# Longer attention rings, earlier batch norm rows and earlier routing breaks in a four-layer graph network

## The chip, the cores and the metric

The kernel runs on one core of one Trainium2 chip. A core has five engines that run side by side, each through its own list of instructions in order: TensorE (PE, with its weight loads as PEld), VectorE (DVE), ScalarE (ACT), GpSimd (POOL) and SyncE (SP). SP issues the plain transfers, GpSimd the gathers and scatters by index. The metric is the device time of one launch in microseconds (us), the median of the runs.

## The reference

Four layers work on x, 3125 tokens by 256 columns (f32, 25 tiles of 128 rows). Each layer does

    xn = layernorm(x)
    x  = x + gnn(xn, edges) + mix(xn)
    x  = x + ffn(...)

with a different gnn, mix and ffn each time. Two pieces matter here. Layer 1's gnn is graph attention with 4 heads of 64 columns over 50000 edges: per edge a score, a softmax over the edges of a destination, and a weighted sum of the source rows. Layer 3's ffn has 4 experts of hidden width 512; which two experts a token uses, and with what weight, comes out of another graph attention, with 4 heads of 4 columns over 32768 edges of its own:

    h     = (x @ W_gat) as (tokens, 4 heads, 4 experts)
    e     = leaky_relu(a_src[src] + a_dst[dst]); alpha = softmax of e over the edges of a dst
    agg   = segment_sum(h[src] * alpha, dst) + b_gat
    score = layernorm(agg).mean over heads; w = softmax of the best 2
    x     = x + sum over experts of w * (gelu(xn @ W1 + b1) @ W2 + b2)

Layers 2 and 3 have a batch norm over all tokens at the end of their gnn, before relu and the addition to x.

## The kernel before, in words

**Edges come in chunks of 128**, sorted by destination: 391 chunks for the graph, 256 for the routing list. For each chunk GpSimd gathers the 128 source rows from DRAM into SBUF by one indirect transfer, VectorE makes a one-hot matrix of destinations (E, L455), and TensorE adds one-hot times rows into a PSUM bank (L459, to_windows). When the last chunk that touches a tile of 128 tokens is in, the tile is closed.

**Attention with a ring (gat_near, from L832).** Gathered rows live in a ring of RING = 35 chunk slots. Iteration i of the generator asks for chunk i (L892), and works chunk i - late, late = 30: it multiplies the rows by their softmax weight (L904) and sums them. Between the two, scores are worked in batches of 16 chunks (CB): batch b starts at iteration 16b + 24, 8 after its last row is asked for, and takes six steps, one per iteration: scores plus leaky relu (L856, L858, DVE), a transpose (L862, PE), two running maxima along the sorted edges (L868, L870, DVE), a transpose back (L879, PE), exp (L884, ACT). A gather may overwrite a slot only when the sum of the chunk that was there, 35 earlier, is done. The running maxima need "breaks": penalties of -2^100 wherever the destination changes (breaks, L787), computed from a list of destinations in DRAM (dlin) with 4 SP loads per 5 batches (L803) and two VectorE instructions (L805, L806).

**Order of work.** A generator yields pieces, and drive() takes turns between generators: (gat_near, 4), (experts, 3) means four iterations of the ring, then three steps of the experts. GpSimd's instructions keep the order of the program. The other engines' instructions are ordered when the kernel is built, by readiness and by place in the program, and what stands inside an If cannot move out of it.

**The last stage (tail_regular, L2299)** runs inside such an If. It holds, in program order: small loads; bn_end (scale and shift of the batch norm from the sums); breaks for the routing list; l3_near_setup; bn_apply, which per group of up to four tiles loads the normalised-to-be rows of the batch norm from DRAM into xn (L1034), scales, shifts, adds them to x (L1036 to L1039), layer-norms and transposes the group, and through fill() makes its 24-column rows (L116 with wg), writes them to DRAM (l3rows, the table the ring gathers from) and scatters the destination scores (l3seed); 12 steps of the experts; the spread of destination scores along the edges (spread, L824, L827); 40 more steps; and then ring and experts in turn. The groups go in the order 16, 20, 24, 0, 4, 8, 12 (first tile); tiles 16 to 24 have no routing edges, so their gates are known at once.

**The experts (l3_near_ffn, L2240)** go through the token groups in that order. For each expert there are 4 steps of hidden layer (product, Gelu on ACT, L2264) and one output step per tile (product, then x += gate * product on DVE, L2275), then the bias (L2289 to L2294). Before the output steps of a group the generator waits, in program order, until the group's gates are there (ready). The last group (12) keeps its products and adds them when its gates come.

**Layer 3's gnn stage** drives seg_near (gather and sum of 391 chunks, 2 per round), l3_mix (1 per round) and route_check (1 per round), which after 12 rounds loads the sorted routing list, writes its destinations to dlin2 and tests that the list has the regular form; the test decides the If.

Of the kernel before, what the change touches and what calls it, by code (L numbers as in the profile page):

```python
# [38 lines left out]
RING = 35  # L39
# [61 lines left out]
class Net:  # L101
# [685 lines left out]
    def breaks(self, pool, dlin, n):  # L787
# [10 lines left out]
        with self.tc.tile_pool(name="br", bufs=1) as tmp:  # L798
            for b0 in range(0, nb, 5):
                k = min(5, nb - b0)  # L800
                dh = tmp.tile([4 * CB, 5, w], F32, name="dh", bufs=2)[:, :k]
                for h in range(4):
                    nc.sync.dma_start(dh[h::4],  # L803
                                      self.lin(dlin, b0 * CB * P, [[P, CB], [CB * P, k], [1, w]]))
                nc.vector.tensor_tensor(pen[:, b0:b0 + k, 1:w], dh[:, :, 1:], dh[:, :, :w - 1], op=OP.not_equal)  # L805
                nc.vector.tensor_scalar(pen[:, b0:b0 + k, 1:w], pen[:, b0:b0 + k, 1:w], -BIG, None, op0=OP.mult)  # L806
            w = P + HALO
            dh = tmp.tile([per, 4, w], F32, name="dhc")
            nc.sync.dma_start(dh, self.lin(dlin, 0, [[P, per], [per * P, 4], [1, w]]))
            nc.vector.tensor_tensor(penc[:, :, 1:], dh[:, :, 1:], dh[:, :, :w - 1], op=OP.not_equal)  # L810
            nc.vector.tensor_scalar(penc[:, :, 1:], penc[:, :, 1:], -BIG, None, op0=OP.mult)
# [20 lines left out]
    def gat_near(self, pool, g, table, pre, pen, d, close):  # L832
# [5 lines left out]
        n, late = g["n"], CB + 14  # L838
        f = d + 2
        nb = -(-n // CB)  # L840
        ring = pool.tile([P, RING, 4, f], F32, name="ring")
        att = pool.tile([P, nb * CB + 2, 4], F32, name="att")
        ex = pool.tile([P, nb * CB, 4], F32, name="ex")
        nc.vector.memset(att, 0.0)

        def spans(c0, c1):
            while c0 < c1:
                e = min(c1, c0 - c0 % RING + RING)
                yield c0, e, ring[:, c0 % RING:c0 % RING + e - c0]
                c0 = e  # L850

        def batch(b):
# [31 lines left out]
            nc.scalar.activation(ex[:, c0:c0 + CB, :], dif, AF.Exp)  # L884
# [5 lines left out]
        for i in range(n + late):  # L890
            if i < n:
                nc.gpsimd.indirect_dma_start(out=ring[:, i % RING].rearrange("p h f -> p (h f)"), out_offset=None,  # L892
                                             in_=table,
                                             in_offset=bass.IndirectOffsetOnAxis(ap=g["src"][:, i:i + 1], axis=0))
            for b in range(nb):
                if i == min(b * CB + CB, n - 1) + 8:
                    live.append(batch(b))
# [4 lines left out]
            if c >= 0:  # L902
                r = ring[:, c % RING]
                nc.vector.tensor_mul(r[:, :, :d + 1], r[:, :, :d + 1],  # L904
                                     ex[:, c, :, None].to_broadcast([P, 4, d + 1]))
# [122 lines left out]

    def bn_apply(self, b, sc, sh, then=None, order=GROUPS):

        nc = self.nc
        for t0, n in order:
            h = self.xn[:, t0:t0 + n, :]
            nc.sync.dma_start(h, b["h"][t0 * P:(t0 + n) * P, :].rearrange("(t p) f -> p t f", p=P))  # L1034
# [1077 lines left out]
    def route_check(self, pool, table, ok):  # L2112

        nc = self.nc
        for _ in range(12):
            yield
# [10 lines left out]
        self.none_bad(pool, bad, ok)  # L2127

# [170 lines left out]
    def tail_regular(self, sorted_r, bn, gb):  # L2299
# [4 lines left out]
        with tp("g3") as gp, tp("ffn3") as fp, Banks(self, mm=4, ga=2, seg=2):  # L2304
            r = gp.tile([P, T, 4], F32, name="r")
            nodeg = gp.tile([P, T], F32, name="nodeg")
            par = {n: self.rowb(gp, "L3_ffn_" + n) for n in ("b_gat", "ln_gamma", "ln_beta")}
# [3 lines left out]
            sc, sh = self.bn_end(bn, fp, *gb)  # L2311
            pen, penc = self.breaks(gp, self.dlin2, C2)
            with tp("set4") as p:
                g, rows_d, aself, gin, pre, fill, end = self.l3_near_setup(gp, p, sorted_r)
                nc.vector.tensor_scalar(nodeg, self.deg2, 0.5, -BIG, op0=OP.is_lt, op1=OP.mult)

                def gate(t0, n):
                    self.l3_gates(gp, gin, par, r, t0, n)
                    ready.add(t0)

                def then(t0, n):
                    fill(t0, n)
                    if t0 >= T2:
                        gate(t0, n)
                self.bn_apply(bn, sc, sh, then, GROUPS[4:] + GROUPS[:4])
                for _ in range(12):
                    next(experts)
            with tp("spread4") as p:
                end(p, penc)
            for _ in range(40):  # L2330
# [7 lines left out]
            drive((self.gat_near(gp, g, rows_d, pre, pen, 4, close), 4), (experts, 3))  # L2338
# [146 lines left out]
    def fast(self):  # L2485
# [3 lines left out]
        with tc.tile_pool(name="keepf", bufs=1) as keep, tc.tile_pool(name="dramf", bufs=1, space=DRAM) as dram:  # L2489
# [41 lines left out]
            with tp("att1") as gp:  # L2531
# [13 lines left out]
                with Banks(self, mm=2, acc=2, ga=2, seg=2), tp("mix1") as mp:  # L2545
                    close = self.gat_close(gp, table, 64, aself, nodeg, 1e-12, add_x)
                    drive((self.gat_near(gp, g, table, pre, pen, 64, close), 4), (self.l1_mix_lean(mp), 1),
# [27 lines left out]
            with Banks(self, **norms), tp("bn2") as bp:  # L2575
                with tp("gl2") as gp:
# [10 lines left out]
                    sc, sh = self.bn_end(bn, bp, self.rowb(gp, "L2_gnn_gamma"), self.rowb(gp, "L2_gnn_beta"))  # L2587
                self.bn_apply(bn, sc, sh)
# [20 lines left out]
            with tp("bn3") as bp:  # L2609
                gb = [self.rowb(bp, "L3_gnn_" + k) for k in ("gamma", "beta")]  # L2610
                bn = self.bn_start(bp)
                with Banks(self, **norms):
                    with tp("gl3") as gp, tp("mix3") as mp, tp("chk4") as cp:
                        drive((self.seg_near(gp, g, tab, g["src"], self.l3_close(gp, own, bn)), 2),
                              (self.l3_mix(mp, self.xnT), 1), (self.route_check(cp, by_dst, ok4), 1))
# [5 lines left out]
                with branch.Else():  # L2621
                    with Banks(self, **plain), tp("end3") as p:
                        self.bn_apply(bn, *self.bn_end(bn, p, *gb))
# [262 lines left out]
```

## Time and profile before

| | |
|---|---|
| runs before | 5095.69, 5095.82, 5095.60 us; median 5095.69 |
| profiled execution | 5092.92 us, span 5091.2 us |
| granted TensorE clock, mean | 0.798 |
| busy: PE, DVE, ACT, POOL | 3585.0, 2165.8, 879.8, 2586.8 us |
| layer 1's ring: first and last gather | 1230.4, 1821.4 us |
| last stage: first expert loads to the end | 4318.8 to 5091.2 us |
| routing ring: first and last gather | 4415.8, 4997.3 us |

How to read it: an engine's busy time is a mean over stages that are limited by different things, so the stretches that the change touches are read one by one: what each engine did there, and what ended its idle time. A line such as "L892 POOL DMA_INDIRECT ring<-l3rows,e2src x256 | busy, mean ns | idle <- releaser" names the line of the code, engine, operation, what is written from what, how often, the busy time, and the idle time just before these instructions with what ended most of it. "remote" and "issue" are waits whose cause the trace does not show. One TensorE product in f32 appears as two instructions.

### The profile page before, as it was taken

Reading aid. Unit: us, or ns where it says so; the run is one execution under the profiler, and the core shown is the slowest. Engines: PE = TensorE matmul, PEld = TensorE weight load, DVE = VectorE, ACT = ScalarE, POOL = GpSimd, SP = SyncE. Lnnn points to the kernel's source line nnn. Section 1 sums busy time; section 2 is a strip of 40 time slices with the busy share of each in tenths; the row PEclk is TensorE's granted clock in tenths of the full one; section 3 lists DMA queues with packets and bytes.
Section 4 is the critical chain, followed back from the end, with each engine's and each line's share of the span. In section 5 each row is a group of like instructions: output and inputs, shape, how many; then the busy total and the mean of one; then the engine's idle time right before and its main releaser. Section 6 shows DMA issues by size and latency. Waiting matters only on the chain. (4 is left out here: it accounts for less than half of the span.)

```text
span 5091.2 us, 45299 instructions
## 1 busy us (share of the span) xinstructions
PE 3585.0 (70%) x12927; PEld 2341.1 (46%) x12927; DVE 2165.8 (43%) x7507; ACT 879.8 (17%) x1815; POOL 2586.8 (51%) x2609
## 2 busy tenths in 40 slices
PE   8657655864765666675766669998677885585779
PEld 3345433542433434343555434555455553354556
DVE  3565321125676774574434342113544223423333
ACT  2010001110210111112201021221112221211222
POOL 0565665664677735443666624660454445305540
PEclk9878767975877877777877779999788987586779
DMA  3422323313433320012333310001233223300000
GB/s 142 125 86 79 92 76 109 98 50 108 129 93 97 101 58 17 15 47 69 97 98 111 107 32 7 14 9 42 82 87 91 72 75 91 85 6 13 12 11 10
DMA packets 231338, 349.01 MB, mean 69 GB/s; under 512 B 74144, under 2 KB 168151, under 8 KB 231080
## 3 DMA queue, kind: packets, MB, share of 16 engines
q0 software_dynamic: 108384, 219.50, 15.7%
q1 hardware_dynamic: 118280, 122.48, 7.7%
q10 hardware_dynamic: 4416, 4.01, 0.2%
q8 instruction: 110, 1.80, 0.1%
q14 instruction: 148, 1.21, 0.1%
HBM read 295.13 MB, written 50.61 MB: 68 GB/s over the span
## 5 line engine op out<-in xcount | busy, mean ns | idle before, releaser
L494 POOL DMA_INDIRECT G<-tab,e1src x391 | 381.1, 975 | 489.9 <-PE seg L459 211.5
L459 PE MATMUL seg<-G,E 128*128 128x257 f32 (+1 forms) x1564 | 472.2, 441 | 213.5 <-DVE E L455 77.1
L116 PE MATMUL mm<-xnT,w 128*128 128x512 f32 (+1 forms) x1232 | 550.2, 595 | 10.9 <-DVE x L1937 4.5
L370 POOL DMA_INDIRECT by_src<-rec,place x391 | 399.1, 1021 | 310.9 <-PE mm L116 204.5
L494 POOL DMA_INDIRECT G<-h_tab,gi x391 | 379.5, 971 | 347.0 <-DMA selfw<-in_L_gnn_self_W 122.9
L455 DVE TENSOR_SCALAR E<-iota_row,e1dl 128x128 f32<-128x128 f32 x1173 | 327.7, 300 | 509.6 <-PE seg L459 252.6
L892 POOL DMA_INDIRECT ring<-l1rows,e1src x391 | 434.8, 1112 | 157.6 <-issue 81.6
L459 PE MATMUL seg<-ring,E 128*128 128x264 f32 (+1 forms) x1294 | 385.4, 427 | 181.9 <-DVE E L455 79.6
L459 PEld LDWEIGHTS seg<-G,E 128*128 128x128 f32 x1564 | 323.4, 219 | 344.5 <-issue 170.5
L494 POOL DMA_INDIRECT G<-tab,e3src x391 | 384.1, 982 | 190.3 <-issue 77.2
L116 PE MATMUL mm<-w,hT 128*128 128x256 f32 (+1 forms) x1712 | 439.0, 409 | 29.9 <-ACT hT L1602 21.2
L892 POOL DMA_INDIRECT ring<-l3rows,e2src x256 | 243.1, 950 | 339.7 <-PE seg L459 125.2
L459 PEld LDWEIGHTS seg<-ring,E 128*128 128x128 f32 x1294 | 245.4, 236 | 299.6 <-DVE E L455 119.3
L116 PEld LDWEIGHTS mm<-w,hT 128*128 128x128 f32 (+1 forms) x1712 | 333.4, 201 | 104.0 <-ACT hT L1602 30.0
L370 POOL DMA_INDIRECT by_dst<-rec,place x256 | 251.5, 983 | 243.1 <-PE mm L116 184.5
L116 PEld LDWEIGHTS mm<-xnT,w 128*128 128x128 f32 x1232 | 240.2, 209 | 242.0 <-issue 222.6
L443 PE MATMUL seg<-G,E 128*128 128x256 f32 x1070 | 295.0, 428 | 56.1 <-issue 23.4
L443 PEld LDWEIGHTS seg<-G,E 128*128 128x128 f32 x1070 | 228.9, 218 | 110.1 <-issue 32.3
L431 DVE TENSOR_SCALAR E<-iota_row,e3dl,rec 128x128 f32<-128x128 f32 (+1 forms) x391 | 140.4, 383 | 285.5 <-PE seg L443 142.0
L171 PE MATMUL mm<-ident,xn 128*128 128x128 f32 x400 | 95.0, 398 | 172.9 <-DVE xn L191 103.6
L1762 DVE SCALAR_TENSOR_TENSOR x<-mm,l2t_r,x 128x256 f32<-128x256 f32 x150 | 69.8, 481 | 320.5 <-PE mm L116 282.3
L904 DVE TENSOR_TENSOR ring<-ring,ex 128x260 f32<-128x260 f32 (+1 forms) x647 | 192.7, 318 | 2.7 <-ACT ex L884 2.6
(738 smaller groups left out, 5414.7 us busy)
## 6 DMA issues: line engine op xcount, KB each, us to landing
w<-in_L_ffn_w SPq DMA_DIRECT2D x16, 1024.0 KB
h_tab<-htab_s SPq DMA_DIRECT2D x25, 512.0 KB
r_b<-rowa SPq DMA_DIRECT2D x64, 128.0 KB
bn_h<-c_h SPq DMA_DIRECT2D x50, 128.0 KB
G<-h_tab,gi POOLq DMA_INDIRECT x391
by_src<-rec,place POOLq DMA_INDIRECT x391
ring<-l1rows,e1src POOLq DMA_INDIRECT x391
G<-tab,e3src POOLq DMA_INDIRECT x391
```

Of the source, the lines that this page charges most:

```text
L116: m = self.nc.tensor.matmul(out, l, r, start=(i == 0), stop=(i == last))
L171: self.nc.tensor.transpose(p[:, i * P:(i + 1) * P], src(t0 + i)[:, k * P:(k + 1) * P], self.ident)
L370: return self.nc.gpsimd.indirect_dma_start(out=table, out_offset=bass.IndirectOffsetOnAxis(ap=idx, axis=0), in_=src, in_offset=None, bound ...
L431: self.nc.vector.tensor_scalar(e[:, :w], self.iota2[:, :w], g["dl"][:, c:c + 1], weight[:, c:c + 1], op0=OP.is_equal, op1=OP.mult)
L443: self.nc.tensor.matmul(A[t], e, rows_c, start=first, stop=last)
L455: nc.vector.tensor_scalar(e, self.iota_row, g["dl"][:, c:c + 1], None, op0=OP.is_equal)
L459: nc.tensor.matmul(A["sum"], e, rows_c, start=(c == 0 or window(c - 1, nt) != k), stop=last)
L494: nc.gpsimd.indirect_dma_start(out=ring[i % len(ring)][:, :D], out_offset=None, in_=table, in_offset=bass.IndirectOffsetOnAxis(ap=gidx[:, ...
L892: nc.gpsimd.indirect_dma_start(out=ring[:, i % RING].rearrange("p h f -> p (h f)"), out_offset=None, in_=table, in_offset=bass.IndirectOff ...
L904: nc.vector.tensor_mul(r[:, :, :d + 1], r[:, :, :d + 1], ex[:, c, :, None].to_broadcast([P, 4, d + 1]))
L1762: nc.vector.scalar_tensor_tensor(self.x[:, t, :], p, r[:, t, e:e + 1], self.x[:, t, :], op0=OP.mult, op1=OP.add)
```

## The change

- gat_near takes the size of the ring and the wait from last gather to scores as arguments: 44 slots and 10 in layer 1, 136 slots and 20 in layer 3's routing. late becomes CB + wait + 6: 32 and 42. The softmax weights (ex) live in three rotating tiles of one batch each, no longer in one tile for all.
- The loads of the batch norm's rows become a function, bn_rows. In the last stage it is called first, before bn_end; in layer 2 between bn_end and bn_apply.
- route_check waits no rounds; a new generator tail_setup waits 3 rounds, runs it, and after one more round runs the breaks of the routing list into tiles that live until the last stage, with one dh buffer instead of two.
- In the last stage 4 expert steps are taken after each of the groups 0, 4, 8, 12 of bn_apply (instead of 12 after all), and 24 after the spread (instead of 40).

```diff
-RING = 35
+RING = 44
-    def breaks(self, pool, dlin, n):
+    def breaks(self, pool, dlin, n, bufs=2):
...
-                dh = tmp.tile([4 * CB, 5, w], F32, name="dh", bufs=2)[:, :k]
+                dh = tmp.tile([4 * CB, 5, w], F32, name="dh", bufs=bufs)[:, :k]
...
-    def gat_near(self, pool, g, table, pre, pen, d, close):
+    def gat_near(self, pool, g, table, pre, pen, d, close, size, wait):
-        n, late = g["n"], CB + 14
+        n, late = g["n"], CB + wait + 6
-        ring = pool.tile([P, RING, 4, f], F32, name="ring")
+        ring = pool.tile([P, size, 4, f], F32, name="ring")
-        ex = pool.tile([P, nb * CB, 4], F32, name="ex")
+        EX = {}
...
-            nc.scalar.activation(ex[:, c0:c0 + CB, :], dif, AF.Exp)
+            EX[b] = pool.tile([P, CB, 4], F32, name="ex", bufs=3)
+            nc.scalar.activation(EX[b], dif, AF.Exp)
...
-                if i == min(b * CB + CB, n - 1) + 8:
+                if i == min(b * CB + CB, n - 1) + wait:
...
+    def bn_rows(self, b, order=GROUPS):
+        for t0, n in order:
+            self.nc.sync.dma_start(self.xn[:, t0:t0 + n, :],
+                                   b["h"][t0 * P:(t0 + n) * P, :].rearrange("(t p) f -> p t f", p=P))
     def bn_apply(self, b, sc, sh, then=None, order=GROUPS):
             h = self.xn[:, t0:t0 + n, :]
-            nc.sync.dma_start(h, b["h"][t0 * P:(t0 + n) * P, :].rearrange("(t p) f -> p t f", p=P))
...
     def route_check(self, pool, table, ok):
-        for _ in range(12):
-            yield
...
+    def tail_setup(self, keep, table, ok):
+        for _ in range(3):
+            yield
+        with self.tc.tile_pool(name="chk4", bufs=1) as pool:
+            self.route_check(pool, table, ok)
+        yield
+        self.tail = self.breaks(keep, self.dlin2, C2, 1)
...
     def tail_regular(...):
-        with tp("g3") as gp, tp("ffn3") as fp, Banks(self, mm=4, ga=2, seg=2):
+        pen, penc = self.tail
+        with tp("ffn3") as fp, tp("g3") as gp, Banks(self, mm=4, ga=2, seg=2):
+            order = GROUPS[4:] + GROUPS[:4]
+            self.bn_rows(bn, order)
+            sc, sh = self.bn_end(bn, gp, *gb)
...
-            sc, sh = self.bn_end(bn, fp, *gb)
-            pen, penc = self.breaks(gp, self.dlin2, C2)
...
                 def then(t0, n):
                     fill(t0, n)
                     if t0 >= T2:
                         gate(t0, n)
+                    else:
+                        for _ in range(4):
+                            next(experts)
-                for _ in range(12):
-                    next(experts)
...
-            for _ in range(40):
+            for _ in range(24):
                 next(experts)
...
-            drive((self.gat_near(gp, g, rows_d, pre, pen, 4, close), 4), (experts, 3))
+            drive((self.gat_near(gp, g, rows_d, pre, pen, 4, close, 136, 20), 4), (experts, 3))
...
-                    drive((self.gat_near(gp, g, table, pre, pen, 64, close), 4), (self.l1_mix_lean(mp), 1),
+                    drive((self.gat_near(gp, g, table, pre, pen, 64, close, RING, 10), 4), (self.l1_mix_lean(mp), 1),
...
+                self.bn_rows(bn)
                 self.bn_apply(bn, sc, sh)
...
-                              (self.l3_mix(mp, self.xnT), 1), (self.route_check(cp, by_dst, ok4), 1))
+                              (self.l3_mix(mp, self.xnT), 1), (self.tail_setup(bp, by_dst, ok4), 1))
```

## The prediction, made before the changed kernel ran

> **What bounds the kernel now.** I read the page first, then GpSimd's waits in the last stage, then engine time by stretch, then the timeline around the start of that stage. On the page, two groups are the gathers that the rings hold:
>
> ```profile
> L892 POOL DMA_INDIRECT ring<-l1rows,e1src x391 | 434.8, 1112 | 157.6 <-issue 81.6
> L892 POOL DMA_INDIRECT ring<-l3rows,e2src x256 | 243.1, 950 | 339.7 <-PE seg L459 125.2
> ```
>
> In layer 1 GpSimd is idle little more than the 0.30 us that stands between any two gathers; in layer 3's routing it idles longer (339.7 us) than it works. Its waits there, and the two gathers around the longest of them (timeline):
>
> ```profile
> POOL ring L892 <- PE seg L459: 125.2, 24, 28.8
> POOL ring L892 <- DVE x L2275: 118.5, 2, 115.2
> ```
> ```profile
> 4459.01 0.94 POOL L892 DMA_INDIRECT ring<-l3rows,e2src  x1 [0.30 <-issue]
> 4575.20 0.94 POOL L892 DMA_INDIRECT ring<-l3rows,e2src  x1 [115.24 <-DVE x L2275]
> ```
>
> After 35 gathers the ring is full. The first slot comes free only when chunk 0 is summed, and that sum stands on TensorE behind the expert products: 115.2 us with no gather. What follows is the price. Columns: stretch, length, busy time of PE, PEld, DVE, ACT, POOL, granted clock, DMA share, GB/s:
>
> ```profile
> 4460.00:4575.00 115.00, 103.43 (x365) 68.57 (x365) 26.37 (x72) 20.64 (x30) 0.00 (x0) 0.89 0.02 5
> 4575.00:4711.00 136.00, 77.75 (x368) 62.15 (x367) 49.28 (x295) 25.68 (x57) 78.01 (x83) 0.67 0.09 13
> 4711.00:4771.00 60.00, 57.41 (x221) 37.87 (x221) 24.56 (x115) 13.96 (x23) 27.16 (x29) 0.90 0.07 7
> 4771.00:4840.00 69.00, 39.53 (x151) 29.62 (x150) 23.31 (x158) 12.09 (x24) 40.78 (x44) 0.62 0.10 17
> 5024.00:5091.00 67.00, 61.27 (x226) 40.47 (x225) 25.51 (x107) 23.55 (x32) 0.00 (x0) 0.96 0.05 17
> ```
>
> Dense stretches (PE busy over 90%, clock 0.89 to 0.96) alternate with stretches in which PE has no expert product to do, because the next token group's gates need chunks that are not there. There GpSimd runs at its own pace (44 gathers in 69 us) and the clock falls to 0.62. So the last 516 us are bound by TensorE in part and by gathers that started too late in part.
>
> The head of the stage, from the timeline:
>
> ```profile
> 4320.33 14.62 SPq L803 DMA_DIRECT2D dh<-dlin  x16
> 4328.68 1.22 DVE L805 TENSOR_TENSOR pen<-dh 64x1035 bf16<-64x1035 f32 x1
> 4335.67 1.15 SPq L1034 DMA_DIRECT2D xn<-bn_h  x2
> 4341.01 1.21 DVE L1036 TENSOR_TENSOR xn<-xn,bn_sc 128x1024 f32<-128x1024 f32 x1
> ```
>
> The batch norm rows are asked for only after 16 loads for the breaks, and are first scaled at 4341.0, though scale and shift were ready at 4328.8.
>
> **Part by part.** The profiled execution took 5092.92 us, its span is 5091.2; the median is 5095.69. I subtract from the median what I take off the span.
>
> *Steps of the experts.* A 4-tile group is 33 steps of the generator, the 1-tile group 21, in all 219. Four hidden-layer steps are 16 products in 7.03 us, four output steps 32 in 7.07: 1.76 us a step. Before: 12 + 40 steps, then 3 per 4 chunks; chunk 0 is summed at iteration 30 (7 rounds, 21 steps), behind 73. After: 4 x 4 + 24, and iteration 42 (10 rounds, 30 steps): behind 70. Late scoring therefore costs nothing there.
>
> *Head.* The breaks go from SP and DVE, and the rows go first: 4341.0 becomes about 4328, 13 us earlier. Against it, 16 expert steps now stand between the groups of the batch norm. One group's PE work there is 2.2 + 3.7 us (the transposes and L116 with wg, at clock 0.51) in some 8 us; four steps add 7 to 14 us. At worst each of the last three groups is 12 us later (36 in all), at best none. I take 10, nearer the best, since DVE, not PE, fills that stretch (47.6 against 45.9 us of 74): the first gather comes at 4413 instead of 4415.8, with 16 steps done.
>
> *Spread.* Now 4417.6 to 4472.9. In it ACT L2264 waits 43.7 us in four pieces for something the trace does not name, and each frees a PSUM bank that the spread needs. Clean, it is four scans at 2.33 plus the load, about 15 us; dirty, 55 as now. I take 35: over at 4450. Then 54 steps (95 us) and one bias round (6.4): chunk 0 at 4552 to 4555, instead of 4574.6. **Gain 20** (bounds -25 and 45).
>
> *Ring of 136.* By then gathers have gone on without a pause at 1.25 us: (4553 - 4413) / 1.25 = 112 chunks ahead. All 256 could be there by 4413 + 320 = 4733. What paces the chunks then? The row for scored chunks: at 4681.09, 32 instructions (16 chunks) in 7.02 us; from the scores' product (4672.38) to that point 8.7 us. With no overlap (8.7 + 7.0) / 16 = 0.98 us a chunk. Now 42 chunks take 69 us from 4642 to 4711, 1.64 each. Group 0's gates need chunks 0 to 66. PE's part: bias 6, the 1-tile group 17, its bias 1.5, group 0's first hidden layer 7, 28 chunks between them at 0.33 plus scores 12: 44 us; then 39 chunks at 0.98: 38. Together 82 us, instead of 137. **Gain 55** (bounds 27, where 1.64 stays, and 77, where PE alone, 60 us, is left).
>
> *Groups 4 and 8* each have such a stretch, 69 us of 129, for 41 chunks. At 0.98 that is 40 plus 9 for the first hidden layer: gain 20. As the rows are there early, 44 of 64 chunks can go between expert steps (now about 25), which leaves 20: gain 35. I take 30 each, **60** (bounds 0 and 80). The last 121 us are dense already: 0.
>
> *Layer 1, ring 44.* From 1291 to 1822, 356 gathers took 531 us: 391 busy, 107 in gaps of 0.30, 33 of other waiting, most for PE seg. The lead of a gather over the slot it reuses grows from 5 to 12 chunks (7 to 18 us; the longest wait is 7.6). Scores two chunks later cost 3 us at the end. **Gain 25** (bounds -3 and 33). The new three-buffer ex tile is written again 48 chunks later and read for 16: no wait.
>
> *Layer 2's rows* were asked for from 2654.7 to 2945.9 already, before scale and shift: 0. *Breaks inside layer 3*: 7 us of DVE and 15 of SP issue, and with one dh buffer SP waits for DVE three times; behind it stand the rows of l3_close. GpSimd waits 164 us for PE sums there and DVE idles 205 us before its one-hots, so they hide it: 0; without that cover, up to 15.
>
> Sum: 20 + 55 + 60 + 25 = 160; 5095.7 - 160 = **4936 us**.
>
> [...] DVE's one-hot (L455, tensor_scalar) waits for unnamed events 11 times, 22.4 us, between 4640 and 4720, up to 5.8 us, while gathers run back to back. [...]
>
> **Rivals.** *Gathers hold up the other engines* (20%). From 4415 to 4460 PE was busy 18.6 of 45 us at clock 0.71, 0.29 of full pace; from 4751 to 4772, with gathers equally dense, about 0.9. From first gather to end PE has some 426 us left (experts 310 after 16 steps, 1-tile group 17, biases 20, sums 256 x 0.23, scores 16, spread 4). Gathers take 320 at least. At pace f beside them the end comes 320 + 426 - 320 f after the first: 653 us at 0.29 against 676 now. With layer 1's 25 that is 5048; at f = 0.45, 4996. I set 5025.
>
> *The same, and slower than before* (11%): below f = 0.22 the stage is longer than now, since the long ring removes the pause in which TensorE ran freely (4460 to 4575). At f = 0.1 it takes 714: 38 more, nothing from layer 1: 5134. For it: the four waits of ACT. Against it: 57.4 busy us of 60 from 4711.
>
> *Handoffs, not gathers, pace the chunks* (13%): 1.64 us stays, the two later stretches give nothing, the first 27: 5095.7 - 20 - 27 - 25 = 5024. For it: the chain L862, L868, L870, L879, L884, L904 crosses engines five times per 16 chunks. Against it: 16 chunks in 7.02 us.
>
> **How the numbers follow.** The forecast has 56%: its bounds give 4885 to 5000. With the two rivals below the old time the range is 4880 to 5050, which leaves out the slower case, some of the dirty contention and a little below. A measurement tells 0.2%, 10 us. Faster 0.86 (0.56 + 0.20 + 0.13 less 0.03 at the edge), same 0.03, slower 0.11.
>
> **What would show it.** Right: no GpSimd gap over 10 us among the first 136 l3rows gathers; all 256 issued by about 4760; chunk 0 summed 10 to 40 us earlier; in the stretches before group 0, 4 and 8 under 1.1 us a chunk and a clock over 0.7; first L1036 of the tail 10 to 13 us sooner; layer 1's gathers at 1.42 us or less. Wrong: expert products at half pace as long as gathers run, or stretches without expert products as long as now although the rows lie ready.

## The result, and the profile after

The new kernel takes 5160.27 us (median of eight runs), the kernel before 5095.65 on the same chip: a ratio of 1.0131, with a 95% interval of 1.0094 to 1.0168. It is slower by 1.3%; the forecast was 4936 us. The profiled execution has a span of 5152.5 us against 5091.2. The 61 us more are spread like this (us, from the first or last instruction of each kind in the two traces):

| stretch | before | after | difference |
|---|---|---|---|
| start to layer 3's first gather | 3592.5 | 3593.0 | +0.5 |
| layer 3's gathers, first to last | 708.1 | 744.7 | +36.6 |
| last gather of layer 3 to first of the routing | 115.1 | 120.2 | +5.1 |
| first routing gather to the first sum over the ring (chunk 0) | 158.8 | 257.8 | +99.0 |
| that sum to the end | 516.6 | 436.8 | -79.8 |

So the long ring did make the chunks quicker once they began, but they began 99 us later, and layer 3 lost what the rest won. The two rings on the page of the new kernel (columns as before):

```profile
L894 POOL DMA_INDIRECT ring<-l1rows,e1src x391 | 438.6, 1122 | 158.3 <-issue 85.0
L894 POOL DMA_INDIRECT ring<-l3rows,e2src x256 | 246.4, 962 | 221.2 <-DVE x L2289 84.9
```

Layer 1's ring of 44 idles as long as that of 35 did (157.6). In the routing the idle time fell from 339.7 to 221.2 us, and the 115 us pause after 35 gathers is gone: the first 136 follow each other in 172.5 us. But TensorE stands still beside them. Engine time by stretch (stretch, length, busy time of PE, PEld, DVE, ACT, POOL, granted clock, DMA share, GB/s):

```profile
4458.00:4500.00 42.00, 19.34 (x68) 12.09 (x66) 7.94 (x9) 3.40 (x6) 32.86 (x31) 0.74 0.14 25
4500.00:4550.00 50.00, 12.74 (x20) 5.20 (x20) 3.04 (x10) 1.97 (x3) 37.81 (x41) 0.60 0.08 10
4550.00:4600.00 50.00, 11.53 (x35) 8.47 (x35) 0.48 (x1) 2.06 (x3) 37.81 (x41) 0.57 0.08 10
4600.00:4650.00 50.00, 0.88 (x2) 0.50 (x2) 1.73 (x4) 0.00 (x0) 23.79 (x26) 0.50 0.06 6
4650.00:4700.00 50.00, 47.66 (x154) 29.62 (x154) 13.11 (x52) 9.67 (x14) 0.00 (x0) 0.88 0.03 11
```

From 4500 to 4650 PE is busy 25 of 150 us. It comes back to life at 4650, when GpSimd has stopped. What VectorE did meanwhile, from its timeline:

```profile
4504.30 0.27 DVE L857 TENSOR_TENSOR att<-ring,pre 128x64 f32<-128x64 f32 x1 [19.26 <-DMA ring<-l3rows,e2src]
...
4524.35 0.26 DVE L857 TENSOR_TENSOR att<-ring,pre 128x64 f32<-128x64 f32 x1 [18.35 <-DMA ring<-l3rows,e2src]
...
4544.35 0.27 DVE L857 TENSOR_TENSOR att<-ring,pre 128x64 f32<-128x64 f32 x1 [19.08 <-DMA ring<-l3rows,e2src]
...
4582.29 0.48 DVE L2289 SCALAR_TENSOR_TENSOR x<-mm,r,x 128x256 f32<-128x256 f32 x1 [37.42 <-remote]
4604.69 0.48 DVE L2289 SCALAR_TENSOR_TENSOR x<-mm,r,x 128x256 f32<-128x256 f32 x1 [21.91 <-remote]
4627.09 0.48 DVE L2289 SCALAR_TENSOR_TENSOR x<-mm,r,x 128x256 f32<-128x256 f32 x1 [21.92 <-remote]
4646.69 0.48 DVE L2289 SCALAR_TENSOR_TENSOR x<-mm,r,x 128x256 f32<-128x256 f32 x1 [19.12 <-remote]
```

Two different troubles stand here. Up to 4544, VectorE waits three times some 19 us for gathered rows: the first add of a batch's scores (L857) stands in its list, 16 more gathers have to land, and the expert sums behind it wait too. After that it adds expert products (L2289) at 4582, 4605 and 4627, 22.4 us apart, and at 4647, and no instruction in the trace explains why. PE's last such product had ended at 4569.6:

```profile
4560.63 8.93 PE L116 MATMUL mm<-w,hT 128*128 128x256 f32 x26 [9.27 <-ACT hT L2278]
...
4649.12 1.22 PE L2307 MATMUL mm<-b,rT 4*128 4x256 f32 x2 [64.91 <-DVE rT L2305]
```

By the profile the data for the adds at 4582, 4605, 4627 and 4647 were thus complete at 4569.6. What came late was the signal from PE: it is on record at 4582.27 for the first of them. I call the first trouble W (a wait for data, by VectorE's order) and the second H (PE's signals held up).

### The profile page after: what moved, and what is told of

It reads as the page before. It is cut to its first block, busy times and chain, and to the rows that moved or that the text cites. A ratio compares the mean times of both kernels' runs of the same rounds, so it can differ in the third digit from the quotient of the medians.

```text
span 5152.5 us, 45178 instructions
## 1 busy us (share of the span) xinstructions
PE 3596.1 (70%) x12927; PEld 2334.0 (45%) x12927; DVE 2161.5 (42%) x7488; ACT 887.8 (17%) x1822; POOL 2603.3 (51%) x2609
## 4 chain that ended last, share of the span: by engine, by line
PE 54%; DVE 16%; another core or an unknown queue 12%; issue 10%; DMA 3%; POOL 3%; ACT 2%; SPq 1%; POOLq 0%; DVEq 0%; ACTq 0%
PE mm L116 32%; PE seg L459 10%; PE seg L443 4%; DVE E L455 2%; POOL ring L894 1%; DVE ring L906 1%; PE mm L171 1%; DVE ln_st L180 1%; PE mm L997 1%; POOL G L494 1%; PE bn L1006 1%; DVE r_m L2100 1%; PE ga L863 1%; PE mm L1421 1%
## 5 line engine op out<-in xcount | busy, mean ns | idle before, releaser
L459 PE MATMUL seg<-G,E 128*128 128x257 f32 (+1 forms) x1564 | 481.1, 446 | 215.8 <-DVE E L455 104.7
L459 PE MATMUL seg<-ring,E 128*128 128x264 f32 (+1 forms) x1294 | 385.0, 425 | 155.7 <-DVE E L455 71.7
L459 PEld LDWEIGHTS seg<-G,E 128*128 128x128 f32 x1564 | 324.4, 220 | 354.4 <-issue 152.2
L116 PE MATMUL mm<-w,hT 128*128 128x256 f32 (+1 forms) x1712 | 426.7, 403 | 52.1 <-ACT hT L2278 30.4
L894 POOL DMA_INDIRECT ring<-l3rows,e2src x256 | 246.4, 962 | 221.2 <-DVE x L2289 84.9
L459 PEld LDWEIGHTS seg<-ring,E 128*128 128x128 f32 x1294 | 231.9, 229 | 276.5 <-DVE E L455 125.0
```

The costliest lines, as they stand in the source:

```text
L116: m = self.nc.tensor.matmul(out, l, r, start=(i == 0), stop=(i == last))
L459: nc.tensor.matmul(A["sum"], e, rows_c, start=(c == 0 or window(c - 1, nt) != k), stop=last)
L894: nc.gpsimd.indirect_dma_start(out=ring[:, i % size].rearrange("p h f -> p (h f)"), out_offset=None, in_=table, in_offset=bass.IndirectOff ...
```

## The experiments

Nothing but the kernel differs within one group of runs, and every ratio is to the kernel before on the same chip. The chips were of two kinds, which matters below: on kind A the kernel before took 5093 to 5160 us (the chip of the result is one, 5095.65), on kind B 4516 to 4523.

**The handoff by itself (kind A).** A kernel of ten stretches, without the network; in short, with names simplified:

```diff
+for _ in range(40):                    # one handoff pair
+    nc.tensor.matmul(p, ident, h, start=True, stop=True)
+    nc.scalar.copy(h, p)
+for c in range(64):                    # beside it
+    nc.gpsimd.indirect_dma_start(out=ring[:, c], in_=table, ...)
+    nc.gpsimd.memset(fill[:, :256], 1.0)   # "filled" only
```

> Leaves out the whole network: it only measures the disputed cost by itself, in ten stretches one after the other. In each a chain of 40 handoffs runs (a 128x512 product on PE, its copy on ACT, the next product from that copy), beside something else: nothing; 64 gathers of 96-byte rows back to back; the same with a fill of 256 columns on GpSimd after each; with a fill of 2048 columns after each eighth; 64 gathers of 1 KB rows; 64 plain transfers asked for by SP; GpSimd filling memory without any gather; gathers beside a chain of PE and VectorE; gathers beside a chain of VectorE and ACT without PE; gathers again beside 80 handoffs. Theory H (back-to-back gathers hold up the signals by which one engine releases another): a handoff pair takes about 2.3 us alone and 10 us or more while gathers are issued without a break, so that the burst's 80 us pass with some 10 pairs; with a fill after each gather it is near 2.5 us. Rival W (the stretch of the new kernel waited on the gathers' own data, in the order of VectorE's list): no chain here uses a gather's data, so each runs at the pace of the one alone, within 20%. [...]

Alone a pair takes 2.75 us. Beside unbroken gathers (one each 1.25 us) it keeps that pace for 48 us, 38 gathers, and from then on takes 5.60 us. ACT's timeline in the stretch "burst":

```profile
160.56 0.58 ACT L177 COPY h_burst<-p 128x512 f32<-128x512 f32 x1 [2.16 <-issue]
163.46 0.58 ACT L177 COPY h_burst<-p 128x512 f32<-128x512 f32 x1 [2.31 <-PE p L170]
169.05 0.58 ACT L177 COPY h_burst<-p 128x512 f32<-128x512 f32 x1 [5.01 <-remote]
174.65 0.59 ACT L177 COPY h_burst<-p 128x512 f32<-128x512 f32 x1 [5.01 <-remote]
```

The product before the copy at 169.05 had ended at 166.2 on PE; its signal is on record at 169.03. And the copies of some stretches as groups (idle time and what ended it behind the second bar):

```profile
L177 ACT COPY h_burst<-p 128x512 f32<-128x512 f32 x40 | 23.4, 585 | 106.0 <-PE p L170 54.2 <-remote 34.4 <-issue 17.3
L177 ACT COPY h_filled<-p 128x512 f32<-128x512 f32 x40 | 23.4, 585 | 86.6 <-PE p L170 86.6
L177 ACT COPY h_pool<-p 128x512 f32<-128x512 f32 x40 | 23.4, 585 | 86.6 <-PE p L170 86.6
```

A fill of 0.33 us after each gather (1.44 us apiece) ends the hold-up entirely; so does one of 1.82 us after each eighth (mean 1.44). GpSimd's fills without gathers leave the pair at 2.75. So do 64 plain transfers from SP; they ran beside the stretch with a fill after each eighth gather, not in one of their own. Gathers of 1 KB rows hold up like those of 96 bytes (24.4 us of "remote" waits against 34.4), and a chain of PE and VectorE is held up too (32.9 us). So on this chip it is PE's signals that are held up, at one per 5.6 us, beside gathers that go on unbroken. The 22.4 us between the adds above are four times 5.6, and four products make one expert sum; that the one comes from the other is not shown. The size was not the one I expected (10 us or more from the start).

How many gathers it takes is not fixed. In the three stretches in which handoffs and gathers begin together it is 35 to 39. The last stretch goes on gathering where the one before stopped, so its handoffs begin 48 us into a run, and still keep their pace for 21 us, up to the 56th gather. In the network it can take far fewer: in the kernel before, such waits stand beside the first 35 routing gathers (from 4415.8), the first of them within 18 gathers. ACT in the last stretch, and in the kernel before:

```profile
1015.06 0.58 ACT L177 COPY h_again<-p 128x512 f32<-128x512 f32 x1 [2.16 <-PE p L170]
1023.70 0.58 ACT L177 COPY h_again<-p 128x512 f32<-128x512 f32 x1 [5.01 <-remote]
```
```profile
4438.33 0.69 ACT L2264 ACTIVATE hT<-mm,b 128x512 f32<-128x512 f32 x1 [19.90 <-remote]
4446.02 0.69 ACT L2264 ACTIVATE hT<-mm,b 128x512 f32<-128x512 f32 x1 [7.00 <-remote]
4457.22 0.69 ACT L2264 ACTIVATE hT<-mm,b 128x512 f32<-128x512 f32 x1 [10.51 <-remote]
```

VectorE need not be in the chain for this: pairs of PE and ACT alone go from 2.75 to 5.60 us. In the chain of VectorE and ACT something smaller shows: a step takes 1.11 us beside the first gathers and then 1.25, the gathers' own pace, as VectorE's copies go from 0.43 to 0.57 us:

```profile
949.07 0.43 DVE L172 COPY p_nope<-h_nope 128x512 f32<-128x512 f32 x1 [0.68 <-ACT h_nope L177]
953.73 0.57 DVE L172 COPY p_nope<-h_nope 128x512 f32<-128x512 f32 x1 [0.69 <-ACT h_nope L177]
```

**Undoing one part at a time (kind A, with the above).** The old ring in the last stage; the check and the breaks where they were; and the long ring as the only change to the kernel before (the calls alone; the comments are mine):

```diff
-(self.gat_near(gp, g, rows_d, pre, pen, 4, close, 136, 20), 4)     # first run, in the new kernel
+(self.gat_near(gp, g, rows_d, pre, pen, 4, close, 35, 8), 4)
-(self.tail_setup(bp, by_dst, ok4), 1)                              # second run, in the new kernel
+(self.route_check(cp, by_dst, ok4), 1)   # after 12 rounds; breaks after bn_end again
-(self.gat_near(gp, g, rows_d, pre, pen, 4, close), 4)              # third run, in the kernel before
+(self.gat_near(gp, g, rows_d, pre, pen, 4, close, 136, 20), 4)
```

> The new kernel with the ring of the last stage back at 35 chunks and scores 8 steps after their batch, all else as in the new one. Theory H: the last stage no longer has 173 us of unbroken gathers, so the first sum over a ring comes some 80 to 100 us earlier after the stage's start (255 instead of 356 us), the later groups lose about 80 us again (129 us for 64 chunks instead of 99); the stage as a whole is 10 to 30 us shorter than the new kernel's, the whole 5125 to 5150 us. Rival W and rival P (the placing of the expert steps, 16 inside the scaling and 24 after the spreading, is what starves TensorE): nothing changes before the first sum, and the later groups still lose, so the whole is 50 to 80 us longer than the new kernel.

> The new kernel with the check of the routing list and its breaks back where they were: the check stepped late in layer 3, the breaks at the head of the last stage. Theory M (the move made layer 3 longer): the last gather of layer 3 comes some 37 us earlier, the head of the last stage is 10 to 15 us longer, the whole 20 to 30 us shorter than the new kernel, near 5135 us. Rival N (layer 3 differs by chance of the order, not by the move): layer 3 stays within 10 us of the new kernel's, and the whole gets 10 to 15 us longer.

> The kernel before with one part of the change alone: the ring of 136 chunks and scores 20 steps after their batch in the last stage; layer 1 keeps its 35. Theory H: layer 3 is as in the kernel before; from the first gather of the last stage to the first sum 230 to 260 us pass (159 in the kernel before), the later groups take 99, 87 and 121 us; the whole is 0 to 30 us longer than before, 5095 to 5125 us. Rival W': without the moved steps the long ring does what it was forecast to do: first sum after 100 us, whole 4960 to 5000 us.

| | ratio (95%) | layer 3's gathers | first gather to first sum | first sum to end |
|---|---|---|---|---|
| before | 1 | 708.1 | 158.8 | 516.6 |
| new kernel | 1.0131 (1.0094 to 1.0168) | 744.7 | 257.8 | 436.8 |
| ring of 35 | 0.9991 (0.9970 to 1.0012) | 745.4 | 123.0 | 515.7 |
| check and breaks back | 1.0036 (1.0010 to 1.0062) | 712.3 | 258.1 | 430.6 |
| long ring alone | 1.0071 (1.0044 to 1.0098) | 713.5 | 280.9 | 430.7 |

In these runs the ring makes the late first sum wherever it is long (258, 258, 281) and nowhere else. With the ring of 35 the other edits bring the first sum 36 us sooner than before; ACT's waits for late signals ahead of it, four in the kernel before, are gone. From the first gather to the end it is 56 us shorter than the new kernel (expected 10 to 30), so the ring did more harm than I had put it at; the chunks after the first sum lose the 79 us again, as expected. The early check and breaks cost layer 3 its 33 to 37 us, and only there: with both back in their place the head of the last stage was not longer (114.9 us against 120.2). Inside layer 3 the loss lies between gathers 100 and 150. GpSimd's waits there, from 3771 to 3854 in the new kernel, and for as long in the one with the parts back:

```profile
POOL G L494 <- PE seg L459: 43.1, 10, 21.1
```
```profile
POOL G L494 <- PE seg L459: 22.7, 12, 6.6
```

The gathers wait for sums that stand on PE behind a block of the mix's products (from 3786 on): another order of the lists. That it is the place and not the work, the next runs show.

**Repairs one and two: fills, and a later place in layer 3 (kind B).** A fill after each of the first 136 gathers of the last stage; tail_setup after 80 rounds; both; and a sweep of paces for the handoffs:

```diff
+                if d == 4 and i < 136:
+                    nc.gpsimd.memset(self.idle[:, :256], 0.0)
-        for _ in range(3):
+        for _ in range(80):
             yield
```

> The new kernel with one thing added: after each of the first 136 gathers of the last stage GpSimd fills 256 columns of a spare tile, 0.33 us each by the run of handoffs alone, so that a gather is asked for every 1.44 us instead of every 1.25. Theory H (after some 38 unbroken gathers one signal of PE gets through in 5.6 us): the hold-up goes, TensorE is dense from 4500 us on, the first sum over a ring comes 200 to 260 us after the stage's start instead of 356, and the whole is 60 to 130 us shorter than the new kernel, 5030 to 5100 us, although GpSimd does 45 us more work. Rival W (the wait on the gathers' own data in VectorE's order) and rival P (too few expert steps beside the gathers): the last of the 136 gathers lands 26 us later, so the first sum comes no earlier and the whole is 0 to 30 us longer than the new kernel.

> The new kernel with the routing check and the breaks still inside layer 3, but after 80 steps of it instead of 3. Theory M1 (they push the mixing's and the closing's products apart where they are put early, gathers 100 to 150): layer 3's gathers take 708 to 718 us instead of 745, the whole is 25 to 37 us shorter than the new kernel, 5123 to 5135 us. Rival M2 (their work costs layer 3 that much wherever it lies): 735 to 750 us from first to last gather, the whole within 10 us of the new kernel.

> Both edits together: the fills after the first 136 gathers of the last stage, and the check and the breaks after 80 steps of layer 3. Theory H with M1: the two add up, 5000 to 5070 us, faster than both kernels. Rivals W and M2: 5150 us or more.

> Leaves out the whole network: 75 handoffs between PE and ACT (2.75 us each alone) beside 128 gathers, eight times, with another pace each: no fill; a fill of 32, of 128 columns after each gather; of 256 columns after each second, each fourth, each eighth; of 2048 columns after each 16th, each 32nd. Theory Q (gathers asked for every 1.25 us run ahead of what carries them out, the lead fills up after some 38 of them, and PE's signals wait from then on): it depends on the mean pace alone; paces from about 1.4 us on are free, with less fill the hold-up begins later than 48 us, in proportion to 1 over what is missing. Rival G (any gap lets the waiting signals through): even one small fill in 8 ends the hold-up, whatever the mean pace, and then signals come through once per gap.

The sweep shows no hold-up at any pace, 128 unbroken gathers at 1.25 us included: kind B does not have H. The ratios were 1.0181 (1.0159 to 1.0203) with fills, 1.0059 (1.0036 to 1.0083) with the later place, 1.0086 (1.0062 to 1.0110) with both. The later place is worth 44 us in layer 3's gathers (580.9 against 625.0; expected 27 to 37). The fills bring the first sum 23 us sooner and lengthen what follows by 33 us, a net loss, where there is no H to mend. They also change the order of VectorE's list (three expert sums move ahead of score adds), and its waits for gathered data fall from 139.5 to 114.4 us. But without fills the first sum still came 204 us after the first gather, with H absent. VectorE's waits from the first gather to the first sums in the run with the later place, without fills:

```profile
DVE att L857 <- DMA ring<-l3rows,e2src: 139.5, 9, 19.3
```

That is W, nine times. The reason is the list itself. In the order in which VectorE's instructions were built, with expert sums as x, score adds as ATT and chunks as mul, the last stage begins:

```
before:  x2 se1 x2 se3 ATT3 x12 SCAN2 mul16 x16 mul15 ATT1 ...
new:     x8 se4 ATT2 x3 ATT1 x1 ATT1 x4 SCAN1 ATT1 SCAN1 mul16 ATT1 x2 ATT1 x2 ...
```

A ring of 35 has rows for two batches and the start of a third before a chunk is summed, so later adds can't stand early. The ring of 136 allows it, and the order, which is fixed when the kernel is built, puts them ahead of expert sums that TensorE is waiting for, although 16 gathers take 20 us.

**Repair three: the adds held back (kind A).** The add depends on the last chunk multiplied before it in the program, on the same engine:

```diff
+                    self.tc.add_manual_dep(v, done[-1], info, reason="after the chunks so far")
```

> The new kernel with one thing added: in the last stage the add that begins a batch's scores on VectorE is ordered behind the last chunk worked on before it in the program, so that VectorE's list no longer has six of these adds, each waiting for 16 more gathers, ahead of the second batch of chunks. Nothing else moves; the gathers run as far ahead as in the new kernel. Theory W (VectorE stands in front of data that lands 20 us a batch, with the expert sums queued behind): the first sum over a ring comes 60 to 120 us after the first gather instead of 204 to 258, the whole is 40 to 120 us shorter than the new kernel, a ratio to before of 0.985 to 1.005. Theory H alone (only PE's held-up signals count): where the signals are held up, the first sum stays 200 us or more after the first gather and the whole within 15 us of the new kernel.

> The same, and the check and the breaks after 80 steps of layer 3 instead of 3. Theory W with M1: 30 to 47 us shorter than the one with the scores held back alone, ratio to before 0.975 to 0.995.

> The same, and a fill of 256 columns after each of the first 136 gathers. Theory H: on a chip that holds up PE's signals after some 38 unbroken gathers this is 10 to 60 us shorter than without the fills; on one that doesn't, 0 to 15 us longer.

> The new kernel with the old ring of 35 and wait of 8 in the last stage, and the check and the breaks after 80 steps of layer 3: what is left of the change when its two harmful parts are taken out. Theory: the last stage is 20 to 40 us shorter than in the kernel before (the rows first, expert steps under the scaling, no breaks at its head), layer 3 as before; ratio to before 0.992 to 0.997. If the long ring with held scores is worth anything, the one with the scores held back and the late check is faster than this one.

| | ratio (95%) | first gather to first sum | first gather to end |
|---|---|---|---|
| adds held back | 1.0141 (1.0109 to 1.0173) | 258.2 | 716.0 |
| and later place | 1.0076 (1.0046 to 1.0106) | 257.6 | 718.3 |
| and fills (first 136) | 0.9975 (0.9951 to 0.9999) | 122.5 | 653.1 |
| ring of 35, later place | 0.9942 (0.9919 to 0.9965) | 123.3 | 643.4 |

The later place is worth 26 us here (expected 30 to 47). On a chip with H, holding the adds back alone changes nothing in the first sum, against W's expectation: the data waits go, and PE's late signals take their place. The kernel with the adds held back, from first gather to first sum:

```profile
DVE x L2292 <- remote: 156.1, 6, 66.7
ACT ex L889 <- DVE dif L887: 83.7, 1, 83.7
ACT hT L2281 <- remote: 83.3, 4, 51.9
```

With the fills added, the expert sums wait for PE's work and no longer for its signal, and PE is dense beside the gathers, 38.77 of 40 us at clock 0.86:

```profile
DVE x L2294 <- PE mm L116: 73.4, 22, 10.5
```
```profile
4533.00:4573.00 40.00, 38.77 (x120) 23.03 (x119) 9.80 (x40) 8.32 (x11) 35.29 (x55) 0.86 0.12 22
```

This pair tells H apart on kind A: one fill of 0.33 us per gather moves the first sum from 258 to 122 us. In VectorE's list the fills move the first score add behind three expert sums; that add waits 9.87 us without them and 10.14 with them, so this is not what makes the difference. Of the 135 us, 70 are lost again after the first sum (530.6 us to the end against 460.7), where the gathers past the 136th have no fills. Yet the ring of 35 is as good (0.9942), and it beats both kernels.

**What a long ring is worth, and whether the other layers pay too (kind B).** The sweep again (it fell on kind B once more), fills after all 256 gathers of the last stage with the long ring and held adds, the same fills with the ring of 35, and fills (two of 64 columns) after every gather of every layer with both rings at 35:

> Leaves out the whole network; the same sweep as before (75 handoffs of 2.75 us between PE and ACT beside 128 gathers: no fill; 32, 128 columns after each gather; 256 after each second, fourth, eighth; 2048 after each 16th, 32nd), because the first one fell on a chip without any hold-up. On a chip with it: theory Q (mean pace) has the hold-up begin after 38 to 45 gathers without a fill and with 32 columns (1.25 and 1.26 us), later with 256 after each eighth (1.27) and fourth (1.30), and not at all from 1.34 us on. Rival G (any gap lets signals through): all stretches with a fill are free, whatever their pace.

> The new kernel with the scores held back, the check and the breaks later, and the fill of 256 columns after each of the 256 gathers of the last stage, not only after the first 136. If the later gathers still hold up TensorE: 10 to 40 us shorter than with the first 136 filled alone, ratio to before 0.990 to 0.996. If TensorE is the bound after the first sum: the same within 10 us, 0.996 to 1.000.

> The same fills with the ring of 35 and the wait of 8 in the last stage (no scores held back). If the later gathers hold up TensorE: 10 to 40 us shorter than the ring of 35 without fills, ratio to before 0.986 to 0.993. If not: 0.992 to 0.997 as without. Against the long ring with the same fills it shows what the length of the ring is worth with both troubles gone: nothing, if the two are within 10 us.

> The ring of 35 in the last stage and in layer 1, the check and the breaks later, and two fills of 64 columns after every gather of all four layers and the last stage. If the kernel before paid for held-up signals in its layers too (ACT and VectorE waits that nothing recorded ends, some hundreds of us in the gather stretches): 50 to 200 us shorter than before, ratio 0.96 to 0.99. If those waits were off the path, or the gathers set the pace of the layers: 0 to 60 us longer than before.

The sweep: no hold-up at any pace, as before, so the pace from which H sets in is not known beyond this: 1.25 us has it, 1.44 has not. Long ring with all repairs: 0.9860 (0.9837 to 0.9883), first sum 117.2 us after the first gather, 394.9 from there to the end. Ring of 35 with fills: 0.9975 (0.9957 to 0.9994), 127.6 and 436.6. So on kind B the long ring is worth some 42 us after the first sum. Chunks 28 to 66 come at 1.27 us apiece, in a later run of the same kernel at 0.96. Against the kernel with fills and the later place (180.9 us to the first sum, on another chip of kind B) only the held adds differ up to the first sum: they take off 64 us, which is the price of W there. Fills everywhere: 1.2114 (1.2089 to 1.2138), far off both expectations. Two small fills cost more than one of 256 columns, as the next gather mostly starts 0.55 us after them, against 0.17 after the one:

```profile
199.59 0.95 POOL L494 DMA_INDIRECT G<-h_tab,gi  x1 [0.52 <-PE seg L459]
200.55 0.37 POOL L497 MEMSET idle<- 128x64 f32 x2
201.47 0.95 POOL L494 DMA_INDIRECT G<-h_tab,gi  x1 [0.55 <-PE mm L116]
```

At 1.88 us a gather layer 0's gathers take 749 us instead of 517: there the gathers set the pace. The last stage follows them too: against the ring of 35 with one fill, its last gather comes 81 us later (550.7 against 469.7 us after the first) and its end 79 us (643.6 against 564.3). What kind A loses to H in the layers this run can't tell. That the layers have such waits there is on record: in the new kernel on kind A ACT waits some 400 us and VectorE some 530 us for "remote" before the last stage, and on kind B, in the next group, neither does once. How much of that lies on the path is not shown.

**Both once more (kind B).** The long ring with all repairs, and the new kernel unchanged:

> The new kernel with the scores held back, the check and the breaks later, and the fills after all 256 gathers of the last stage, once more. On a chip that holds up PE's signals: if both causes are the whole of it, the first sum comes some 122 us after the first gather, the whole 40 to 80 us shorter than the new kernel and 10 to 40 us shorter than the kernel before, ratio 0.992 to 0.998; if something else slows the long ring there, 0.998 or more. On a chip without the hold-up: 0.984 to 0.989 again.

> The new kernel unchanged, for its time on the same chip. On a chip that holds up PE's signals: ratio to before 1.009 to 1.017 again, first sum 250 to 260 us after the first gather. On a chip without the hold-up: VectorE's waits for gathered data remain (a first sum 200 to 205 us after the first gather) and layer 3's loss of some 45 us remains, so the ratio is 1.013 to 1.018 there too.

The repaired one has 0.9851 (0.9833 to 0.9868), the new kernel 1.0167 (1.0149 to 1.0184): on kind B it is slower by as much as on kind A, there without H, by W and layer 3 (first sum 204.5 us after the first gather; layer 3's gathers 621.9 against 580 us in the repaired one). The kernel before has no trace on kind B, so whether that is all is not shown. VectorE in the two, from the first gather to the first sums:

```profile
DVE att L857 <- DMA ring<-l3rows,e2src: 139.3, 9, 19.2
```
```profile
DVE att L857 <- DMA ring<-l3rows,e2src: 12.8, 2, 10.0
```

Not tried: on kind A, the long ring with fills on all 256 gathers, and fills without held adds, which would show what W costs there; on kind B, held adds without fills.

## Why the prediction was wrong

- **The ring of 136** is the step that failed. The gathers did go on without a pause as forecast (136 in 172.5 us), and I put chunk 0 some 140 us after the first gather, with nothing of the ring's own before it. It came after 257.8; with the ring of 35 and all else as in the new kernel, after 123.0. I counted the instructions that the long ring moves, not the order of VectorE's list that it makes possible (W), nor what unbroken gathers do to PE's signals (H). In the sum it is the line "54 steps (95 us) and one bias round (6.4)" between the end of the spread and chunk 0: they took 241 us (4474.6 to 4715.7), and 106 us in the kernel with held adds and fills.
- **Where I had the mechanism and gave it too little.** "Gathers hold up the other engines ... below f = 0.22 the stage is longer than now, since the long ring removes the pause in which TensorE ran freely" had 11%. The stage from first gather to end took 694.5 us; by the formula 320 + 426 - 320 f that is f = 0.16, on the slow side of the threshold. What I set for it, ACT's four waits, was H. What I set against it, 57.4 busy us of 60 from 4711, held 29 gathers and hardly a wait for late signals (1.4 us); why that stretch is free of H, no run shows. The two paces behind the formula don't compare, either: 0.29 is PE's busy share times its clock, 0.9 the busy share alone, which times its clock of 0.83 is 0.74.
- **Group 0, 4 and 8.** From the first sum on the gains were 7, 30, 43 and 0 us, 80 in all, against 55, 30, 30 and 0 forecast. The mechanism for the later groups holds; the stretch before group 0 still runs beside gathers (1.58 us a chunk from 4766 to 4845), which the forecast's 0.98 left out. With both troubles taken away on kind B it is 1.27 in one run and 0.96 in another.
- **Head.** The first scaling came 11.4 us sooner after layer 3's last gather (28.9 against 40.3), forecast 13. The 16 expert steps under it cost 16.5 us (91.3 against 74.8 from first scaling to first gather), where I took 10 in bounds of 0 to 36. Together a loss of 5 instead of a gain of 3.
- **Spread.** It was over 16.6 us after the first gather, not 37; the first sum with the ring of 35 was 36 us sooner than before, where I had 20. Right in direction, undersized.
- **Breaks inside layer 3: "they hide it: 0".** They cost 36.6 us, outside my bound of 15. The idle time that I named is real, but an early place changed the order of PE's list, and idle time of VectorE does not cover that. Put after 80 rounds, the same work takes back 44 us on kind B (625.0 to 580.9) and 20 on kind A (757.5 to 737.3); whether some cost is left there, no run on that chip shows.
- **Layer 1's ring of 44:** forecast 25 us, nothing came. From the first gather to the last sum it took 626.9 against 621.6 us. The first sum is 12 us later. The wait that the ring was to take away is still there: GpSimd waits 41.8 us for PE's sums (L459), before 35.1. In the kernel with the long ring alone, layer 1 keeps its 35 slots and takes 623 us, against 626 in the two others of that group that have 44. Why the longer ring brings nothing, no run shows.
- **Layer 2's rows:** 0, as forecast.
- **VectorE's one-hots** (11 waits for unnamed events, 22.4 us) were in no sum. What waited, as far as the run of handoffs shows it, is whoever waits for PE: PE and ACT alone were held up there, at 5.60 us a pair instead of 2.75, and a chain of VectorE and ACT was not. In that last chain VectorE's copies went from 0.43 us beside the first gathers to 0.57 beside later ones, which is small against the 5.60. Whether the one-hots waited for PE, no run shows; whether GpSimd's fills slow VectorE was not tried.

## What to carry to other kernels

A longer buffer also lets the scheduler put consumers early: before counting its gain, read the in-order lists that come of it, and tie an instruction that waits for slow data behind the work that must not wait. A producer that bursts can be slower for the whole than one with small pauses (on kind A here: with held adds the first sum came 258 us after the first gather, and 122 with a fill of 0.33 us after each gather), so test the pace by itself, with a handoff loop beside it. Move covered work only after asking whose order it changes, not only who is idle.

## What the runs showed of the hardware that was not expected

On kind A, beside gathers at 1.25 us without a break, signals of PE reach ACT and VectorE once in 5.60 us. It began after 35 to 39 gathers where handoffs and gathers began together, after 56 where the handoffs began later, and within 18 in the last stage of the kernel before. It lasted 6 to 8 us beyond the last of 64 gathers and 18 us beyond the last of 128. A chain of VectorE and ACT was not held up, nor were the rows late (1.9 us after the last gather). On kind B the same instructions show none of it, and the whole kernel takes 4517 instead of 5095 us. The two kinds differ in one more thing: the trace of the new kernel holds 18,902 records of landed transfers on A and 52,125 on B. In the run of handoffs 239 of 1,024 landings are on record in the held-up burst, and all 1,024 in the filled stretch; but only 647 in the stretch with a fill after each eighth gather, beside SP's 64 transfers, and no signal was held up there. So missing records and late signals do not always go together.

Why the missing landings are not on record, and whether that has to do with the late signals, no run here shows. Every time here comes with a granted clock and so from a recorded execution; that an unrecorded one would be free of H, no run here shows. The cause of H below this level stays open.
